# Macaron stack on one core: the position table's copies go from VectorE to ScalarE, its zeros to GpSimd

## The chip, the cores and the metric

The kernel runs on one core of a Trainium2 chip. The metric is the device time of one execution in microseconds (us), the median over several runs. The core has five engines with a queue of instructions each: TensorE (PE, matrix products; its weight loads are shown as PEld), VectorE (DVE), ScalarE (ACT), GpSimd (POOL) and SyncE (SP), which here only starts transfers. An engine takes its instructions in the order of its queue and waits at one whose semaphores have not come. Sixteen DMA engines carry the transfers that SyncE, ScalarE and GpSimd start. SBUF is the memory on the chip, PSUM the small memory that TensorE writes.

## The reference, cut to what matters

Twelve residual steps in four layers, each a mixture of experts, an attention, and the mixture again. All arithmetic is in 32 bits. The change is in layer 0, on x of 4 x 512 rows of 128:

```python
x = L0_attn_x
x = x + 0.5 * _L0_ffn_ref(_layernorm(x, axis=-1), L0_ffn_gate_w, L0_ffn_w1, L0_ffn_b1, L0_ffn_w2, L0_ffn_b2)
x = x + _L0_attn_ref(_layernorm(x, axis=-1), L0_attn_qkv_w, L0_attn_qkv_b, L0_attn_proj_w, L0_attn_proj_b, L0_attn_rel_pos_emb)
x = x + 0.5 * _L0_ffn_ref(_layernorm(x, axis=-1), L0_ffn_gate_w, L0_ffn_w1, L0_ffn_b1, L0_ffn_w2, L0_ffn_b2)
...
```

`_L0_ffn_ref` is the first mixture: a gate picks one of 8 experts for each row, an expert takes at most 320 rows (`CAP0`), multiplies with w1 (128 x 512), adds b1, takes the ReLU, multiplies with w2 and adds b2. `_L0_attn_ref` is a causal attention of 16 heads that adds to each score a number which depends on the head and on the distance between query and key alone; that number is a sum over `L0_attn_rel_pos_emb`.

## The kernel before, in words

**The table.** The attention reads these added numbers from one SBUF tile, `table`, of 128 partitions x 16 heads x 512 numbers. It is made once, in `prep_table`, at the start of the program and is first read by the attention of layer 0, at about 126 us. Only the last 256 numbers of each head depend on the weights; the first 256 are zero. `prep_table` is a generator with three parts:

- It starts the load of the embedding rows (L1016).
- It sums them (L1021), turns them with one product (L1023) and sends a row of 384 numbers for each head to DRAM (L1031).
- For two heads at a time, eight times in all, it loads the row from DRAM with a shift of one per partition into a tile `rev` of 256 KB (L1037, started by ScalarE), turns the order of the partitions with one product by `flip` into a PSUM bank `turned` (L1042, TensorE), and copies the bank into `table` (L1043, VectorE). Behind the eight it writes the zeros (L1044, VectorE).

The `rev` tiles come from a ring of five SBUF buffers with the tag "raw", which other staging tiles use too; the `turned` banks come from a ring of eight PSUM banks that the whole program uses.

**Around it.** The first mixture's object is `f00`. `f00.tokens` normalizes the rows, computes the gate's choice on VectorE, and GpSimd scatters the rows to the experts' places in DRAM, 16 indirect transfers (L416) in all. The call order is: the second part of the table in the middle of the choices, then the rest of the choices, then the third part of the table, then the transposition of b1 (`b1`, L570 on TensorE, copied into `b1T` by L571 on VectorE), then two memsets of the attention's padded values `vpad` on GpSimd (L585). All this stands in a block with `tc.manual_schedule` for four engines: within it each of them keeps the order in which the Python program issues the instructions.

Behind the block comes `f00.experts`. There SyncE loads an expert's rows `d` (L447); VectorE computes their way back (`lost`, L472, and `back`, L475); TensorE transposes the rows (L466) and ScalarE copies them into `dT` (L468); TensorE makes the hidden layer in four pieces of 128 x 320 (L490), of which ScalarE applies b1 and the ReLU to two (L494) and VectorE to two (L495), both reading `b1T`; TensorE makes the output (L526, `o`), VectorE adds b2 (L506), ScalarE weights it (L511), and GpSimd scatters the result (L512). These instructions are placed by a scheduler, from its own estimate of times, which also moves some of them ahead of instructions that the program issued earlier: on VectorE the `lost` and `back` of the first three experts stand between the first copy of the table and the second.

Of the kernel before, what the change touches and what calls it, by code (L numbers as in the profile page):

```python
# [9 lines left out]
FP = mybir.dt.float32  # L10
# [7 lines left out]
P = 128  # L18
D = 128
NB, S = 4, 512  # L20
# [4 lines left out]
NH = 16  # L25
# [16 lines left out]
def kernel(ctx: ExitStack, tc: tile.TileContext, a: dict, out: bass.AP):  # L42
    nc = tc.nc
# [5 lines left out]
    stage = ctx.enter_context(tc.tile_pool(name="stage", bufs=5))  # L49
# [3 lines left out]
    def const(shape, name, dtype=FP):  # L53
        return cpool.tile(shape, dtype, name=name, tag=name)

    def bank(name):
        return psum.tile([P, 512], FP, name=name, tag="bank", bufs=8)
# [19 lines left out]
    flip = const([P, P], "flip")  # L77
# [934 lines left out]
    def prep_table(pool):  # L1012


        rel = stage.tile([P, D], FP, name="rel", tag="rel", bufs=1)
        nc.sync.dma_start(rel, a["L0_attn_rel_pos_emb"][P - 1 : 2 * P - 1, :])  # L1016
        yield

        table = pool.tile([P, NH, S], FP, name="table", tag="table", bufs=1)
        tab = stage.tile([P, NH], FP, name="tab", tag="tab", bufs=1)  # L1020
        nc.vector.tensor_reduce(tab, rel.rearrange("p (h d) -> p h d", d=HD), AX.X, ALU.add)  # L1021
        ps = bank("tabT")
        nc.tensor.matmul(ps[:NH, :P], tab, flip, start=True, stop=True)  # L1023
        last = stage.tile([NH, 1], FP, name="tab_last", tag="tab_last", bufs=1)
        nc.vector.tensor_copy(last, ps[:NH, 0:1])
        row = stage.tile([NH, 3 * P], FP, name="tab_row", tag="tab_row", bufs=1)
        nc.vector.memset(row[:, :P], 0.0)
        nc.vector.tensor_scalar(row[:, P : 2 * P], ps[:NH, :P], last, None, ALU.subtract)
        nc.vector.memset(row[:, 2 * P :], NEG)
        rows = dram.tile([NH, 3 * P], FP, name="tab_rows", tag="tab_rows")  # L1030
        nc.sync.dma_start(rows, row)  # L1031
        yield

        for h in range(0, NH, 2):

            rev = stage.tile([P, 2, 2 * P], FP, name=f"rev{h}", tag="raw")
            nc.scalar.dma_start(  # L1037
                rev,
                bass.AP(tensor=rows.tensor, offset=rows.offset + h * 3 * P, ap=[[1, P], [3 * P, 2], [1, 2 * P]]),
            )  # L1040
            ps = bank(f"turned{h}")
            nc.tensor.matmul(ps, flip, rev.rearrange("p h s -> p (h s)"), start=True, stop=True)  # L1042
            nc.vector.tensor_copy(table[:, h : h + 2, S - 2 * P :], ps.rearrange("p (h s) -> p h s", h=2))  # L1043
        nc.vector.memset(table[:, :, : S - 2 * P], 0.0)  # L1044
        l0["table"] = table
        yield

# [558 lines left out]
    ps = bank("gate0T")  # L1606
    nc.tensor.transpose(ps[:, :E], gate0, ident[:E, :E])
    nc.vector.tensor_copy(gate0T, ps[:, :E])
    with tc.tile_pool(name="tables", bufs=1) as tables:
        f00 = Mixture("f00", CAP0, 1)  # L1610
        f00.zeroed(stage, "raw", 5)
        made = prep_table(tables)
        next(made)
        whole(f00.empty())
# [144 lines left out]
```

## Time and profile before

| | |
|---|---|
| median of 3 runs | 1507.65 us (1504.37 to 1510.55) |
| the profiled execution | 1506.45 us, its span 1504.7 us |
| PE busy | 1258.4 us, 84% of the span |
| DVE, ACT, POOL busy | 893.8, 685.7, 691.0 us |
| granted TensorE clock, mean | 0.908 |
| chain that ended last | PE 63%, DVE 13%, POOL 9%, issue 7%, DMA 6%, ACT 2% |
| eight loads of `rev` (L1037) | started from 34.21 to 44.8 us |
| eight copies of `turned` (L1043) | 0.68 us each, from 40.4 to 55.3 us |
| zeros of the table (L1044) | 3.47 us, at 56.8 us |

The span runs from the first instruction to the last; the execution's own time is 1.75 us longer. The chain that ended last is followed back from the last instruction, at each step to what released it, or to the instruction before it on its engine; "issue" is time in which the engine waited for nothing that the profile shows. In a line of the timeline stand the start, the duration from the first to the end of the last of the merged instructions, the engine, the line, the operation, what it writes and reads, and in brackets how long the engine was idle before it and what released it. A `q` behind an engine's name marks the starting of a transfer in its queue.

### The profile page before, as it was taken

What the parts mean: (1) busy time and instruction counts of PE and PEld (TensorE: products, weight loads), DVE (VectorE), ACT (ScalarE), POOL (GpSimd) and SP (SyncE); (2) the same over time, 40 slices, a digit from 0 to 9 for tenths busy, and PEclk for the clock granted to TensorE, in tenths of its full rate; (3) what the DMA queues carried; (4) which work ended last, traced back from release to release, by engine and by line L of the source; (5) the groups of instructions that cost most, each with busy time, mean ns of one, the idle gap of its engine ahead of it and who ended that gap; (6) DMA issues with size and microseconds to landing.
All of it is one profiled execution on the core that took longest, in us unless ns stands there. A gap on an engine that the chain in (4) does not pass through costs nothing.

```text
span 1504.7 us, 28029 instructions
## 1 busy us (share of the span) xinstructions
PE 1258.4 (84%) x10133; PEld 787.1 (52%) x10133; DVE 893.8 (59%) x3105; ACT 685.7 (46%) x1438; POOL 691.0 (46%) x810
## 2 busy tenths in 40 slices
PE   4788999995979989998999766439599999998394
PEld 4465666674756656676655334227453334333273
DVE  5326766663345657777467766634277787773243
ACT  2135867871443367776621213104245555564041
POOL 5346767872433678876432112554502224212343
PEclk9998999996999999999999776759799999999597
DMA  9420240002413884241130000032105000000223
GB/s 254 114 60 12 80 171 13 9 5 74 137 52 61 228 259 136 93 141 31 32 80 3 1 1 0 29 92 79 56 8 184 9 11 5 15 2 15 78 82 108
DMA packets 100657, 106.15 MB, mean 71 GB/s; under 512 B 9084, under 2 KB 73832, under 8 KB 100520
## 3 DMA queue, kind: packets, MB, share of 16 engines
q1 hardware_dynamic: 89576, 88.01, 20.3%
q0 software_dynamic: 6656, 13.22, 2.5%
q10 hardware_dynamic: 4288, 3.15, 0.8%
q8 instruction: 80, 1.31, 0.3%
q14 instruction: 57, 0.47, 0.1%
HBM read 62.49 MB, written 41.85 MB: 69 GB/s over the span
## 4 chain that ended last, share of the span: by engine, by line
PE 63%; DVE 13%; POOL 9%; issue 7%; DMA 6%; ACT 2%; SPq 0%; POOLq 0%; DVEq 0%; ACTq 0%
PE s_a L621 13%; PE t_a L666 9%; PE o_f L526 5%; PE h_f L490 5%; PE acc_a L688 5%; PE acc_a L826 4%; DVE x L1450 3%; PE t_a L621 3%; PE y_f L1419 2%; POOL disp_f L416 2%; PE ot_a L845 2%; POOL res_f L512 2%; PE gu_f L1218 1%; PE gu_f L1219 1%; PE T_f L195 1%
## 5 line engine op out<-in xcount | busy, mean ns | idle before, releaser
L653 POOL TENSOR_SCALAR sc_a<-sc_a,top_a 128x128 f32<-128x128 f32 (+3 forms) x256 | 275.8, 1092 | 88.0 <-DVE top_a L638 53.8
L621 PE MATMUL s_a<-k_a,q_a 32*128 32x512 f32 (+3 forms) x1536 | 265.1, 539 | 6.0 <-DVE top_a L642 4.8
L710 DVE TENSOR_REDUCE low<-s_a 128x1 f32<-128x512 f32 x256 | 163.0, 684 | 42.8 <-PE t_a L621 31.0
L730 ACT ACTIVATE w_a<-t_a 128x512 f32<-128x512 f32 x240 | 131.6, 596 | 107.1 <-PE t_a L621 69.2
L666 PE MATMUL t_a<-ident,sc_a 128*128 128x128 f32 x1280 | 171.6, 279 | 7.4 <-DVE top_a L642 6.7
L512 POOL DMA_INDIRECT res_f<-y_f,back_f x112 | 106.6, 952 | 140.1 <-ACT y_f L511 92.3
L666 PEld LDWEIGHTS t_a<-ident,sc_a 128*128 128x128 f32 x1280 | 142.8, 143 | 42.6 <-issue 15.8
L621 PE MATMUL t_a<-ql_a,k_a 32*128 32x512 f32 x480 | 157.9, 640 | 0.4 <-DVE low L710 0.3
L655 ACT ACTIVATE sc_a<-sc_a,top_a 128x128 f32<-128x128 f32 (+3 forms) x256 | 134.7, 575 | 16.1 <-DVE top_a L642 15.6
L621 PEld LDWEIGHTS s_a<-k_a,q_a 32*128 32x128 f32 x1536 | 94.7, 186 | 74.5 <-issue 39.0
L675 ACT ACTIVATE w_a<-t_a 128x256 f32<-128x256 f32 (+2 forms) x192 | 94.3, 526 | 70.4 <-PE t_a L666 70.0
L416 POOL DMA_INDIRECT disp_f<-n_f,to_f x96 | 94.8, 988 | 51.5 <-issue 37.2
L526 PE MATMUL o_f<-w_l,h_f 128*128 128x128 f32 (+1 forms) x896 | 111.9, 280 | 3.6 <-ACT h_f L494 3.6
L526 PEld LDWEIGHTS o_f<-w_l,h_f 128*128 128x128 f32 (+1 forms) x896 | 103.9, 186 | 12.6 <-ACT h_f L494 5.6
L490 PE MATMUL h_f<-dT_f,w_l 128*128 128x320 f32 (+1 forms) x256 | 106.6, 555 | 2.8 <-ACT dT_f L468 2.8
L172 POOL TENSOR_SCALAR rs_f<-mv_f 128x4 f32<-128x4 f32 (+1 forms) x23 | 5.3, 231 | 203.4 <-DVE mv_f L169 202.9
L688 PE MATMUL acc_a<-w_a,vpad 128*32 128x128 f32 x2560 | 97.7, 278 | 0.6 <-ACT w_a L675 0.6
L677 ACT COPY w_a<-t_a 128x256 f32<-128x256 f32 (+2 forms) x192 | 93.5, 526 | 5.7 <-PE t_a L666 5.7
L642 DVE CUSTOM_DVE_ANT_0 sc_a<-s_a,table 128x128 f32<-128x128 f32 (+3 forms) x128 | 62.3, 487 | 46.8 <-PE s_a L621 35.2
L642 DVE CUSTOM_DVE_ANT_0 sc_a<-s_a,future 128x128 f32<-128x128 f32 (+3 forms) x128 | 62.4, 487 | 46.3 <-PE s_a L621 39.5
L511 ACT ACTIVATE y_f<-o_f,d_f 128x128 f32<-128x128 f32 (+1 forms) x112 | 38.9, 394 | 105.2 <-DVE o_f L506 93.5
L826 PE MATMUL acc_a<-w_a,vpad 128*32 128x256 f32 x1024 | 82.5, 391 | 2.7 <-ACT w_a L730 2.3
(338 smaller groups left out, 2200.6 us busy)
## 6 DMA issues: line engine op xcount, KB each, us to landing
fac_a<-fac_a_sb SPq DMA_DIRECT2D x36, 256.0 KB
disp_f<-zeros_f SPq DMA_DIRECT2D x4, 2080.0 KB
d_f<-disp_f SPq DMA_DIRECT2D x32, 260.0 KB
w_l<-in_L_ffn_w_dram SPq DMA_DIRECT2D x16, 512.0 KB
cb_f<-rows_f SPq DMA_DIRECT2D x16, 512.0 KB
q_a<-fac_a SPq DMA_DIRECT2D x32, 256.0 KB
k_a<-fac_a SPq DMA_DIRECT2D x32, 256.0 KB
r_f<-res_f SPq DMA_DIRECT2D x16, 256.0 KB
```

The source lines that it names most:

```text
L416: nc.gpsimd.indirect_dma_start(out=self.to[c][i0 + t][:, :], out_offset=bass.IndirectOffsetOnAxis(ap=to[:, c, t : t + 1], axis=0), in_=ns[ ...
L490: nc.tensor.matmul(ps[u][:, :cap], w1[:, e, (c + u) * P : (c + u + 1) * P], dT, start=True, stop=True)
L512: nc.gpsimd.indirect_dma_start(out=self.back[e * per + s][:, :], out_offset=bass.IndirectOffsetOnAxis(ap=back[:m, s : s + 1], axis=0), in_ ...
L526: nc.tensor.matmul(po[:m, s, :], h[:, c, s * P : s * P + m], w2[:, e, c, :], start=(c == 0), stop=(c == NC - 1),)
L621: nc.tensor.matmul(ps[:, n0:n1], q[r : r + SLOT, i * P : (i + 1) * P], k[r : r + SLOT, n0:n1], start=True, stop=True)
L653: nc.gpsimd.tensor_scalar(sc, sc, top, None, ALU.subtract)
L655: nc.scalar.activation(sc, sc, AF.Exp, bias=top, scale=-1.0)
L666: nc.tensor.transpose(ps[:, x * n + j * P : x * n + (j + 1) * P], st["sc", u, i, r0 + x][:, j * P : (j + 1) * P], ident,)
L688: nc.tensor.matmul(st["acc", u][r * SLOT : (r + 1) * SLOT, i * P : (i + 1) * P], vpads[b % 2][:, j, g * 4 + r, :], st["w", u, i, r][:, j * ...
L710: nc.vector.tensor_reduce(st["low", u][:, i, c : c + 1], ps, AX.X, ALU.max, negate=True)
L730: nc.scalar.activation(w, ps, AF.Exp)
L826: nc.tensor.matmul(acc[r * SLOT : (r + 1) * SLOT, n0:n1], vpads[b % 2][:, j, g * 4 + r, :], st["w", u, j, r, half] if ("w", u, j, r, half) ...
```

## The change

The eight copies are made by ScalarE instead of VectorE. The loads, which ScalarE starts, are now written in between: the first three before the first product, and each further one behind the copy of the part three before it. The zeros are written by GpSimd, whose place for it is behind the 16 scatters of the mixture and in front of the `vpad` memsets. Products, sizes and buffers are the same.

```diff
-        for h in range(0, NH, 2):
-
-            rev = stage.tile([P, 2, 2 * P], FP, name=f"rev{h}", tag="raw")
+
+        revs = {}
+
+        def fetch(h):
+            revs[h] = stage.tile([P, 2, 2 * P], FP, name=f"rev{h}", tag="raw")
             nc.scalar.dma_start(
-                rev,
+                revs[h],
                 bass.AP(tensor=rows.tensor, offset=rows.offset + h * 3 * P, ap=[[1, P], [3 * P, 2], [1, 2 * P]]),
             )
+
+        for h in range(0, 6, 2):
+            fetch(h)
+        for h in range(0, NH, 2):
             ps = bank(f"turned{h}")
-            nc.tensor.matmul(ps, flip, rev.rearrange("p h s -> p (h s)"), start=True, stop=True)
-            nc.vector.tensor_copy(table[:, h : h + 2, S - 2 * P :], ps.rearrange("p (h s) -> p h s", h=2))
-        nc.vector.memset(table[:, :, : S - 2 * P], 0.0)
+            nc.tensor.matmul(ps, flip, revs[h].rearrange("p h s -> p (h s)"), start=True, stop=True)
+            nc.scalar.copy(table[:, h : h + 2, S - 2 * P :], ps.rearrange("p (h s) -> p h s", h=2))
+            if h + 6 < NH:
+                fetch(h + 6)
+        nc.gpsimd.memset(table[:, :, : S - 2 * P], 0.0)
         l0["table"] = table
```

## The prediction

> **What bounds the kernel now.** I read the page first: TensorE is busy 84% of the span and carries 63% of the chain that ended last. The change touches none of its instructions, so what counts is where the head of the program makes TensorE wait. Next the chain of waits in order of time, for the first 260 us:
>
> ```profile
> 42.86 4.04 DMA disp_f<-n_f,to_f
> 47.48 0.48 SPq L447
> 48.00 3.43 DMA d_f<-disp_f
> 51.81 4.19 DVE table L1043 x7
> 56.00 0.80 issue
> 56.80 3.47 DVE table L1044
> 60.35 0.54 ACT h_f L494
> 60.94 3.66 PE o_f L526 x16
> 64.60 1.08 PE h_f L490 x4
> ```
>
> Columns are start, duration, work. From 51.81 to 60.35 the chain runs through VectorE's table work: seven of eight copies (L1043), a gap, the memset (L1044). The activation behind them (L494) needs b1T, whose copy (L571) stands on VectorE behind the memset. From 60.94 on it is TensorE almost alone. Then the timeline of the same place:
>
> ```profile
> 34.21 10.95 ACTq L1037 DMA_DIRECT2D rev<-tab_rows  x8
> 40.44 0.69 DVE L1043 COPY table<-turned 128x512 f32<-128x512 f32 x1 [4.08 <-issue]
> 43.82 1.82 POOL L585 MEMSET vpad<- 128x2048 f32 x1
> 46.53 1.10 PE L1042 MATMUL turned<-rev,flip 128*128 128x512 f32 x2 [0.91 <-DMA rev<-tab_rows]
> ...
> 50.11 0.16 DVE L472 SCALAR_TENSOR_TENSOR lost_f<-d_f,astray 128x3 f32<-128x3 f32 x1 [8.98 <-DMA d_f<-disp_f]
> ...
> 53.39 0.42 ACT L468 COPY dT_f<-dT_f 128x320 f32<-128x320 f32 x1 [24.70 <-PE dT_f L466]
> 53.87 4.11 PE L490 MATMUL h_f<-dT_f,w_l 128*128 128x320 f32 x8 [0.64 <-ACT dT_f L468]
> ```
>
> VectorE copies turned part 0 at 40.44 and then sits 8.98 us, because the `lost` of the experts stands ahead of the other seven copies and waits for d_f. Meanwhile ScalarE does nothing (24.70 idle) and TensorE has turned all parts by 50.07. The transposes of expert 0 start only at 52.6: they take the bank of part 1, copied by 52.41.
>
> **The change part by part.** The order of instructions on each engine differs only here; TensorE's and SyncE's orders are the same, and everything behind the first expert is as before. So the question is by how much the 60.94 to 64.60 step moves.
>
> *Removed from VectorE*: 8 copies of 0.68 and the memset of 3.47, 8.9 us in all, of which 8.5 lay on the chain (51.8 to 60.3). VectorE is then free at 51.8 and its b1T copy waits for TensorE alone.
>
> *Added to ScalarE*: 8 copies of 128x512 from PSUM. Nearest row: its own copy nT (L321), 0.58. 4.6 us in idle time. But they stand in front of the dT copy (L468), and from the fourth load on every load stands behind a copy. This makes a loop that did not exist: a load is issued when a copy is done, the copy waits for its product, the product for its load.
>
> *The loads*. One-microsecond cuts of the timeline put the eight issues of before at 34.2, 34.6, 35.4, 38.4, 40.4, 42.1, 43.9 and 44.8. The fourth waited only for earlier transfers, the fifth to eighth for products 0 to 3 (ended 40.40, 42.1, 43.86, 44.77). The product of load 5 started at 46.53, of load 6 at 48.11, both by a DMA: L = 4.4 and 4.2 us from issue to use, two or three in flight. I take L = 4.2. Here a rule gives less: the Trainium skill, "DMA: Bandwidth & Descriptors", section "Anatomy of one DMA — SWDGE (gpsimd) path", fits a fixed 2.0 us plus the bytes at 436 GB/s, for 256 KB 2.6 us (an estimate; its fit is of GpSimd's path). The trace has 4.2 with the DMA engines 0.73 to 0.92 busy; the trace decides. The d_f load, issued 47.04 and used 50.11, gives 3.1 as the low end.
>
> With a warm product of 1.1 (46.53 to 47.6) and 0.65 from its end to the next issue: copy 0 ends 41.05, load 3 is issued 41.1 (before: 38.4), product 3 45.3 to 46.4, load 6 issued 47.05, product 6 51.25. Copy 1 ends 42.75, load 4 issued then, product 4 46.95 to 48.05, load 7 issued 48.65, product 7 52.85 to 53.95 (before: to 50.07). Two loads follow one another, so each us of L costs 2 us. Then b1 to 54.2, the dT transposes 0.6 to 54.8, ScalarE's last copy to 54.6, dT copied 54.9 to 55.3, first product of expert 0 at **55.4**. That is 1.5 us later than before (53.87); what is late next is the loads.
>
> *What TensorE then takes*. Before, the eight products took 4.11 us, 0.53 each; in later experts four take 1.24, 0.27 apart. And o_f took 3.66, later 1.98 to 2.05. The windows:
>
> ```profile
> 46.00:50.00 4.00, 2.98 (x6) 0.97 (x7) 0.00 (x0) 0.00 (x0) 1.81 (x2) 1.00 0.87 214
> 50.00:54.00 4.00, 0.99 (x6) 0.60 (x6) 3.03 (x10) 0.42 (x1) 0.00 (x0) 1.00 0.66 193
> 54.00:58.00 4.00, 4.00 (x10) 2.49 (x10) 3.20 (x5) 0.00 (x0) 0.00 (x0) 0.57 0.15 42
> 58.00:61.00 3.00, 0.47 (x4) 0.20 (x2) 2.89 (x4) 1.07 (x3) 0.00 (x0) 0.99 0.00 0
> 61.00:65.00 4.00, 4.00 (x19) 3.84 (x20) 0.81 (x2) 0.30 (x1) 0.00 (x0) 0.58 0.00 2
> ```
>
> First number busy PE, then PEld, DVE, ACT, POOL; the third from the end is the granted clock: 0.57 and 0.58 right after gaps of 2.4 us (50.25 to 52.62) and 2.5 us (58.4 to 60.94). The Trainium skill, "TensorE: Matmul & The Clock Gate", section "Why this matters for your kernels", says that gaps up to about 3 us leave the clock up. Both rows contradict it. By the rule the eight products would be warm whatever the gaps; by the rows it depends on the pauses of 1.5 us at most between products 3 to 7, with TensorE busy some 55% of 44 to 55. The nearest row, 46 to 50, busy 75% with pauses of 0.5 to 0.9, kept full speed (products of 0.59). I take warm and keep cold for the range.
>
> Warm: eight products 55.4 to 57.7, dT of expert 1 to 58.1, VectorE's last h at 58.3, o_f in 2.0 from about 58.2 to **60.2**. Before it ended at 64.6: **4.4 us earlier**. Cold: 55.4 to 59.5, transposes to 60.0, o_f (warm by then) to 62.0: 2.6 earlier. The second gap, 58.4 to 60.94, is gone either way, as b1T is ready.
>
> *The zeros on GpSimd.* Its 128x2048 memset takes 1.82, so 128x4096 some 3.6 (between VectorE's 3.47 and 3.65). It runs 43.8 to 47.4 behind the last scatter; the vpad memsets move to 51.5. GpSimd then idles (17.90 us before its scatter at 65.77, some 61 now), so zero; cover left 10 us. Waits of other engines on GpSimd ask for its last count copy before the scatters, not for a memset. The scatters themselves are not moved.
>
> *SyncE* keeps its order, but the raw weight loads behind d_f wait for products 4 to 7: the last two go out at about 54.2 instead of 51.9, and the next d_f behind them waits for expert 0's y (67.45 before). Zero, cover 9 us.
>
> Sum: 4.4 us. The profiled execution was 1506.45 (span 1504.7, 1.75 around it), 1.2 below the median 1507.65, so 1502.05 against itself and **1503.2** against the median.
>
> **The rivals.**
> *A, half the gain (cold clock or slower loads)*: 0 to 3 us, about 1505.5. For it: TensorE is idle nearly half of 44 to 55. Against: the 46 to 50 row.
> *B, the loads come quickly*: L of 3.1 gives 2.2 more, 6.6 in all, 1501; the rule's 2.6 gives 7.6, 1500. For it: fewer loads overlap, so less contention. Against: L stayed 4.2 for the sixth load, too.
> *C, slower: ScalarE's copy-then-load loop becomes the bound.* The loads behind copies stretch until product 7 ends so late that the mixture begins later than the 8.5 us it saves. Price 2 us per us of L; it decides at L = 4.2 + 4.4/2 = 6.4 warm, 5.5 cold. With cold turned products as well (0.85 more each, two in the row), cold o_f (1.7 more) and L 4.4, it is 64.6 - 65.8 = 1.2 slower, 1508.9. For L of 8, cold: 5.0 slower, 1512.7. For: scatters and d_f share the DMA engines, 0.87 busy in 46 to 50. Against: no load here showed over 4.4.
> *D, it doesn't do what it says*: the loads are "three ahead" only for the first three; with d_f landing up to 51.4 the mixture could not start much before anyway. The order shows the copies off VectorE, so only the size is in doubt.
>
> **How the numbers follow.** Likeliest case (2 to 6 us) 0.55; A 0.20; B 0.15; C 0.10. The three runs spread from 1504.37 to 1510.55, so their median is good to some 1.5 us. A measurement of this kernel tells about 0.5%, 7.5 us, from no change. Faster than that needs B at its end plus a lucky median: 0.10. Slower by it needs L above 9: 0.05. Range: 1507.65 - 7.6 - 1.5 = 1498.5 to 1507.65 + 1.2 = 1508.9, taken as 1509.
>
> **What would show it.** L1044 gone from VectorE; GpSimd's memset of 3.6 at about 44; ScalarE's copies of 0.58 from 40.45 with loads between, the last ending near 54.6; first h_f product at 53 to 56; no gap of 2.5 us before the first o_f, which ends near 60.2 and takes 2.0; a chain that runs through load, product, copy from 38 to 55 instead of VectorE. The prediction is wrong if the first o_f ends after 64.6, if expert 0's products are at 0.53 each, or if the time behind 65 us differs by more than the shift.

## The result, and the profile after

The changed kernel takes 1500.82 us (median of 20 runs, 1497.09 to 1505.29) against 1505.49 us for the kernel before on the same chip (20 runs): ratio 0.9969, 95% interval 0.9956 to 0.9982. That is 4.67 us between the medians; 4.4 had been forecast. In a later group the two were run side by side again, with 1507.88 against 1512.2 us, ratio 0.9970 (0.9953 to 0.9987). Both intervals exclude 1, so the gain is real; it is smaller than the 0.5% that the prediction took as what one measurement can tell from no change. (The ratios come from runs side by side on one chip and are not exactly the quotients of the medians. Medians of different groups cannot be compared: those of the kernel before lie between 1494.83 and 1512.2 us.)

The chain of waits of the changed kernel, in order of time (start, duration, work), over the place where the chain before ran through VectorE:

```profile
41.47 4.42 DMA rev<-tab_rows
45.93 1.14 PE turned L1048 x2
47.16 4.05 DMA rev<-tab_rows
51.35 1.10 PE turned L1048 x2
53.83 4.11 PE h_f L490 x8
58.36 1.98 PE o_f L526 x16
60.34 1.08 PE h_f L490 x4
```

VectorE's copies and zeros are gone from it. What leads to the mixture is now load, product, load, product. Expert 0's h products start at 53.83, where they started before (53.87), and take the same 4.11 us. The whole difference comes behind them: o_f follows at once and takes 1.98 us, where before TensorE stood still for 2.5 us and then took 3.66. The next h product starts at 60.34 instead of 64.60: 4.26 us earlier. The lines of the kernel before for that place:

```profile
60.19 0.13 DVE L571 COPY b1T_l<-b_l 128x32 f32<-128x32 f32 x1
60.94 3.66 PE L526 MATMUL o_f<-w_l,h_f 128*128 128x128 f32 x16 [2.53 <-ACT h_f L494]
```

The timeline of the changed kernel, same execution (start, duration, engine, line, work; in brackets the idle time in front and what ended it):

```profile
39.70 0.59 ACT L1049 COPY table<-turned 128x512 f32<-128x512 f32 x1 [11.00 <-DMA rev<-tab_rows]
39.76 0.37 ACTq L1039 DMA_DIRECT2D rev<-tab_rows  x1
41.41 0.59 ACT L1049 COPY table<-turned 128x512 f32<-128x512 f32 x1 [1.12 <-PE turned L1048]
41.47 0.37 ACTq L1039 DMA_DIRECT2D rev<-tab_rows  x1
44.12 3.53 POOL L1052 MEMSET table<- 128x4096 f32 x1
47.52 1.45 SPq L447 DMA_DIRECT2D d_f<-disp_f  x3
51.98 0.16 DVE L472 SCALAR_TENSOR_TENSOR lost_f<-d_f,astray 128x3 f32<-128x3 f32 x1 [15.81 <-DMA d_f<-disp_f]
52.48 0.59 ACT L1049 COPY table<-turned 128x512 f32<-128x512 f32 x1 [2.24 <-PE turned L1048]
53.33 0.18 DVE L571 COPY b1T_l<-b_l 128x32 f32<-128x32 f32 x1
```

Two readings matter here. The load behind a copy on ScalarE goes out 0.06 us after that copy *starts*, not after it ends. And b1T is copied at 53.33, before the h products begin; in the kernel before it came behind the zeros, at 60.19.

The windows (engine busy times as before; third number from the end is the granted clock):

```profile
50.00:54.00 4.00, 2.02 (x7) 0.94 (x8) 1.07 (x7) 1.25 (x3) 1.57 (x2) 0.99 0.71 203
54.00:58.00 4.00, 4.00 (x10) 2.50 (x10) 0.58 (x2) 1.05 (x2) 0.00 (x0) 0.58 0.49 141
58.00:61.00 3.00, 3.00 (x23) 2.60 (x21) 0.95 (x2) 0.59 (x2) 0.00 (x0) 1.00 0.01 2
```

The h products still run at a clock of 0.58; o_f, with no pause before it, runs at 1.00. Below, a stretch of products at the higher speed (h in 2.4 us) is called warm, at the lower one (h in 3.9 to 4.3 us) cold. One product of the table stands in these views as two records (x2).

The profiled spans differ by more than this place: 1494.6 against 1504.7 us. The lead is 4.3 us at 60 us and 4.7 at the first scores of the attention (120.4 against 125.1), then grows further down, where the two kernels execute the same instructions in the same order. Single executions wander by more than the effect (1497.09 to 1505.29 us in the 20 runs of the change on one chip), and the profiled one was the fastest of the 20. The yardstick below is therefore the moment at which the first sixteen o_f products end, counted from the start of the last scatter (L416), since the head of the program itself shifts by some 2 us between executions.

### The profile page after: what moved, and what is told of

The parts are those of the page before. It is cut to its first block, busy times and chain, and to the rows that moved or that the text cites. A ratio compares the mean times of both kernels' runs of the same rounds, so it can differ in the third digit from the quotient of the medians.

```text
span 1494.6 us, 28029 instructions
## 1 busy us (share of the span) xinstructions
PE 1251.1 (84%) x10133; PEld 778.6 (52%) x10133; DVE 885.9 (59%) x3096; ACT 690.7 (46%) x1446; POOL 696.1 (47%) x811
## 4 chain that ended last, share of the span: by engine, by line
PE 63%; DVE 12%; POOL 8%; issue 7%; DMA 7%; ACT 2%; SPq 0%; POOLq 0%; ACTq 0%; DVEq 0%
PE s_a L621 13%; PE t_a L666 9%; PE h_f L490 5%; PE acc_a L688 5%; PE o_f L526 5%; PE acc_a L826 5%; DVE x L1458 3%; PE t_a L621 3%; PE y_f L1427 2%; PE ot_a L845 2%; POOL res_f L512 2%; POOL disp_f L416 2%; PE T_f L195 1%; POOL rstd_f L173 1%; DMA cb_f<-rows_f 1%
## 5 line engine op out<-in xcount | busy, mean ns | idle before, releaser
L416 POOL DMA_INDIRECT disp_f<-n_f,to_f x96 | 95.1, 991 | 51.7 <-issue 36.7
L642 DVE CUSTOM_DVE_ANT_0 sc_a<-s_a,future 128x128 f32<-128x128 f32 (+3 forms) x128 | 62.3, 487 | 45.5 <-PE s_a L621 40.4
```

What stands on the lines that cost most here:

```text
L416: nc.gpsimd.indirect_dma_start(out=self.to[c][i0 + t][:, :], out_offset=bass.IndirectOffsetOnAxis(ap=to[:, c, t : t + 1], axis=0), in_=ns[ ...
```

## The experiments

The measure just described, for all kernels, from their timelines, in us. "h starts" and "o_f ends" are counted from the start of the last scatter.

| kernel | last scatter | h starts | h takes | o_f ends | gain on this measure | ratio to before (95%) |
|---|---|---|---|---|---|---|
| before | 42.86 | 11.0 | 4.11 | 21.7 | | |
| the change | 43.16 | 10.7 | 4.11 | 17.2 | 4.6 | 0.9969 (0.9956 to 0.9982) |
| change_again | 44.93 | 11.2 | 3.87 | 17.5 | 4.3 | 0.9970 (0.9953 to 0.9987) |
| zeros_gpsimd_only | 43.47 | 11.4 | 4.07 | 17.9 | 3.8 | 0.9967 (0.9956 to 0.9978) |
| copies_scalar_only | 44.74 | 11.8 | 4.01 | 18.2 | 3.5 | 0.9969 (0.9955 to 0.9982) |
| zeros_first_vector | 43.94 | 12.3 | 4.16 | 18.9 | 2.9 | 0.9983 (0.9972 to 0.9994) |
| no_loads_ahead | 43.63 | 38.3 | 4.32 | 45.0 | -23.2 | 1.0169 (1.0139 to 1.0198) |
| four_ahead | 44.46 | 8.5 | 4.00 | 14.9 | 6.8 | 0.9914 (0.9888 to 0.9941) |
| four_ahead_again | 44.94 | 8.9 | 4.11 | 15.4 | 6.3 | 0.9943 (0.9921 to 0.9964) |
| filler | 43.01 | 11.3 | 2.42 | 16.1 | 5.7 | 0.9953 (0.9935 to 0.9971) |
| four_filler | 43.73 | 9.2 | 2.42 | 14.0 | 7.8 | 0.9958 (0.9940 to 0.9977) |
| four_filler_again | 43.73 | 11.2 | 2.42 | 16.1 | 5.7 | 0.9952 (0.9933 to 0.9971) |
| four_warm | 44.21 | 11.1 | 2.42 | 15.9 | 5.8 | 0.9945 (0.9928 to 0.9962) |

Each row is one trace, and every gain is counted against the one trace of the kernel before. Two traces of one kernel lie 0.3 us (the change), 0.5 (four_ahead) and 2.1 us (four_filler) apart, so differences of a few tenths say nothing. The gain lasts: at the first scores of the attention, some 60 us later, every kernel has its gain on this measure or up to 0.5 us more.

### Which part of the change earns the gain?

My theory after the two traces was that the change gained one thing: TensorE's pause in front of the first o_f (2.5 us) and the slow clock behind it (3.66 instead of 1.98, 1.7 us). Together they are 4.2 us. The pause goes as soon as b1T is ready before the h products end, and that does not take the whole edit. The rival: the parts add up.

The zeros alone go to GpSimd:

```diff
-        nc.vector.memset(table[:, :, : S - 2 * P], 0.0)
+        nc.gpsimd.memset(table[:, :, : S - 2 * P], 0.0)
```

> One part alone: the table's zeros go to GpSimd, the eight copies and the loads stay as in the kernel before. Measured by the moment at which the first sixteen o_f products end (64.60 us before, 60.34 after the whole change). Theory 'one gap': what the change gained is the 2.5 us pause of TensorE before the first o_f and the cold clock behind it (3.66 instead of 1.98), and it goes as soon as b1T is ready before the h products end at 58. Here VectorE's copies end near 56.0 and b1T follows at once, so the h products run 53.9 to 58.0, o_f about 58.4 to 60.4: the whole 4.2 us with half of the edit. Rival 'parts add up': the copies on VectorE still hold up b1T or VectorE's own activations, o_f begins at 59.5 or later and ends past 62: 2.6 us or less of the gain. Median against before: -4.2 us by the first, -2 by the second.

Its timeline:

```profile
44.43 3.53 POOL L1044 MEMSET table<- 128x4096 f32 x1
52.42 4.27 DVE L1043 COPY table<-turned 128x512 f32<-128x512 f32 x7
54.90 4.07 PE L490 MATMUL h_f<-dT_f,w_l 128*128 128x320 f32 x8 [0.64 <-ACT dT_f L468]
56.61 0.18 DVE L571 COPY b1T_l<-b_l 128x32 f32<-128x32 f32 x1
59.32 2.05 PE L526 MATMUL o_f<-w_l,h_f 128*128 128x128 f32 x16
```

All seven copies are still on VectorE, 52.42 to 56.69. But b1T is there at 56.8, before the h products end at 59, and o_f runs without a pause and warm. Median 1501.55 us against 1506.39, 4.8 us: by the medians as much as the whole change, by the traces 3.8 of its 4.6 us.

The other part alone: the change, with the zeros left on VectorE. They stand in its order where the copies were, and run in its idle time.

```diff
-        nc.gpsimd.memset(table[:, :, : S - 2 * P], 0.0)
+        nc.vector.memset(table[:, :, : S - 2 * P], 0.0)
```

> The other part alone: copies on ScalarE with loads three ahead, the zeros stay on VectorE, where they now stand ahead of the wait for d_f (the copies in front of them are gone). Theory 'one gap': VectorE makes the zeros in its idle time before 42, b1T is copied at about 53.3, and the first o_f ends at 60.3 as with the whole change (gain 4.2). Rival 'parts add up': the zeros' 3.5 us still count somewhere, and o_f ends at 62 or later.

Its timeline:

```profile
38.11 3.47 DVE L1052 MEMSET table<- 128x4096 f32 x1 [0.80 <-issue]
55.38 0.19 DVE L571 COPY b1T_l<-b_l 128x32 f32<-128x32 f32 x1 [0.52 <-PE b_l L570]
56.55 4.01 PE L490 MATMUL h_f<-dT_f,w_l 128*128 128x320 f32 x8 [0.64 <-ACT dT_f L468]
60.91 2.05 PE L526 MATMUL o_f<-w_l,h_f 128*128 128x128 f32 x16
```

The zeros run at 38.11, when VectorE had nothing to do, and nobody waits for them. 1501.5 against 1506.39 us, by the medians again the whole gain, by the traces 3.5 us.

The third moves no work to another engine. One line is put ahead of the loop of copies:

```diff
+        nc.vector.memset(table[:, :, : S - 2 * P], 0.0)
         for h in range(0, NH, 2):
...
-        nc.vector.memset(table[:, :, : S - 2 * P], 0.0)
```

> No work changes its engine: against the kernel before, the line of the zeros on VectorE alone is moved from behind the copies to in front of them. VectorE waits there for product 0 until 40.4 and from 41.1 to 50.1 for d_f, so 3.5 us of zeros fit in front. Theory 'one gap': copies end at 56.0, b1T at 56.1, h products 53.9 to 58.0, o_f ends near 60.4, gain 4.2. Rival 'VectorE's load counts': VectorE must lose the copies too, and o_f ends past 62. If the zeros start late they delay the copy of part 0 by at most 3.5 us, with it load 4, and h begins 1 to 3 us later.

1503.45 us, ratio 0.9983: faster than before, by 2.9 us in the medians and in the trace. That is less than the others by both, but its interval overlaps with theirs. Its timeline:

```profile
53.49 0.16 DVE L472 SCALAR_TENSOR_TENSOR lost_f<-d_f,astray 128x3 f32<-128x3 f32 x1 [0.91 <-DMA d_f<-disp_f]
53.77 4.27 DVE L1044 COPY table<-turned 128x512 f32<-128x512 f32 x7
54.63 0.29 PEld L466 LDWEIGHTS dT_f<-ident,d_f 128*128 128x128 f32 x2 [4.83 <-issue]
60.76 2.05 PE L526 MATMUL o_f<-w_l,h_f 128*128 128x128 f32 x16
```

The pause before o_f is gone here as well (h takes 56.25 to 60.41, o_f follows). But the transposes of expert 0 wait until VectorE has copied part 1, which stands behind the third `lost` (53.49), and in this execution d_f was loaded late (issued 4.98 us behind the last scatter, 4.14 in zeros_gpsimd_only). The difference, 0.84 us, is nearly all of what this kernel's h starts later than that of zeros_gpsimd_only (12.3 and 11.4): where the order on VectorE keeps that link, a late d_f is paid. Why d_f was late one trace can't tell; in change_again it was issued 4.98 us behind the scatter too.

So the parts do not add up. Each one alone gives 2.9 to 3.8 us of the 4.6 by the traces, and two of them the whole by the medians. Of the 8.5 us of VectorE work that lay on the chain, moving the 3.5 us of zeros to GpSimd earned most of the gain or all of it; moving them only within VectorE's own order earned some 60% of it in the one trace, with the late d_f in it.

### The loop on ScalarE

The forecast's rival C was a loop of load, product and copy on ScalarE. Here it is at its purest. Against the kernel before, copies and zeros change their engine and nothing else is edited; since the loads stay where the program had them, each now stands on ScalarE behind the copy before it:

```diff
             ps = bank(f"turned{h}")
             nc.tensor.matmul(ps, flip, rev.rearrange("p h s -> p (h s)"), start=True, stop=True)
-            nc.vector.tensor_copy(table[:, h : h + 2, S - 2 * P :], ps.rearrange("p (h s) -> p h s", h=2))
-        nc.vector.memset(table[:, :, : S - 2 * P], 0.0)
+            nc.scalar.copy(table[:, h : h + 2, S - 2 * P :], ps.rearrange("p (h s) -> p h s", h=2))
+        nc.gpsimd.memset(table[:, :, : S - 2 * P], 0.0)
```

> Copies on ScalarE, zeros on GpSimd as in the change, but no load ahead: each load stands behind the copy before it. This shows what the loop of load, product and copy on ScalarE costs. If a load goes out only when the copy in front of it has ended: eight times (L of 3.4 to 4.2, product 1.1, copy 0.6) is 5.1 to 5.9 each, last product at 34.2 + 8 x 5.5 = 78 (75 to 81). If a load goes out while the copy in front of it still runs (the change's trace has issue and copy start 0.00 to 0.06 us apart): eight times (L + 1.1), 4.5 to 5.3, last product at 70 to 77. The first o_f then ends 6.4 us behind it, at 76 to 87, and the time is 12 to 23 us over that of the kernel before; a rival says that other work (weights, d_f) fills the wait so that it is slower by less than 8.

The chain of waits, three turns of it and the last product:

```profile
52.42 3.15 DMA rev<-tab_rows
55.71 2.06 PE turned L1042 x2
57.86 3.16 DMA rev<-tab_rows
61.06 2.09 PE turned L1042 x2
63.23 3.56 DMA rev<-tab_rows
66.92 2.06 PE turned L1042 x2
...
78.04 2.05 PE turned L1042 x2
```

1530.85 us (4 runs) against 1506.39: 24.5 us slower. A turn is load and product alone, 5.4 to 6.0 us; the copy's 0.59 is not in it, because the next load goes out as the copy starts. The last product ends at 80.1. That lies in the range given for the other reading (75 to 81) and past the one given for this (70 to 77), so the end alone would have told the wrong story; the trace decides. The estimate fell short because it had the product at 1.1 us, and it takes 2.06 where TensorE is busy some 38% of the time (2.06 of 5.4). The rival that other work fills the wait fell.

Next, one turn less instead of more: four loads ahead.

```diff
-        for h in range(0, 6, 2):
+        for h in range(0, 8, 2):
             fetch(h)
...
-            if h + 6 < NH:
-                fetch(h + 6)
+            if h + 8 < NH:
+                fetch(h + 8)
```

> The whole change, but with loads four ahead instead of three, which takes one turn of load and product out of ScalarE's loop. Theory 'two chains meet': in the change's trace the last turned product ends at 52.45 and the last d_f load is used at 51.98, so d_f is next; the last product moves to 49 to 50.5, but the transposes of expert 0 start no earlier than 52 and h at 53.3: the first o_f ends 0.3 to 0.7 us earlier, about 17.0 us behind the start of the last scatter instead of 17.4; nothing that the median can tell from the change. Rival 'the loads are the chain': h starts with the last product, 2 us earlier, o_f ends at 58.3 and the median falls by 2 more.

Here my number was wrong (17.0 us) and the rival's came out (15.1 by its 58.3; measured 14.9), though not by its mechanism: h does not start with the last product. From the timeline:

```profile
47.20 2.81 PE L1048 MATMUL turned<-rev,flip 128*128 128x512 f32 x6 [1.28 <-DMA rev<-tab_rows]
48.99 1.45 SPq L447 DMA_DIRECT2D d_f<-disp_f  x3
51.71 0.61 PE L466 MATMUL dT_f<-ident,d_f 128*128 128x128 f32 x3 [1.52 <-DMA d_f<-disp_f]
52.95 4.00 PE L490 MATMUL h_f<-dT_f,w_l 128*128 128x320 f32 x8 [0.64 <-ACT dT_f L468]
```

The products end at 50, and the transposes wait 1.5 us more for d_f, as I had thought. But d_f comes 2.7 us after its issue, not 4.5: in the change the last load of the table went out 0.36 us ahead of d_f (47.16 and 47.52) and d_f took 4.46. In change_again it was 0.52 ahead, and d_f took 4.32. In the five profiles with four ahead the last table load goes out some 4 us or more ahead of d_f, and d_f took 2.66 to 2.83. Over all 13 profiles it is the same: 4.32 to 4.64 us in the three with a table load 0.36 to 0.52 us in front of d_f, 2.66 to 3.12 in the other ten. So the table's last loads appear to cost twice: as a chain of their own, and by slowing d_f. h starts 8.5 us behind the last scatter instead of 10.7.

The first six runs gave 0.9914 (10.9 us between the medians), more than the 6.8 us of this place. Once more, with the unaltered change beside it (no edit in either):

> The changed kernel once more, unaltered, so that it shares its chip and its runs of the kernel before with the two versions beside it. By its trace (first o_f ends 17.2 us behind the start of the last scatter, 21.7 before) the ratio is 0.9970, 4.5 us.

> Loads four ahead, once more with more runs. By its first trace the first o_f ends 14.9 us behind the start of the last scatter, 6.8 earlier than before and 2.3 earlier than in the change: ratio 0.9954, and 0.9985 of the change. Its first six runs gave 0.9914: if that is so, something behind the first mixture gains 4 us more, and the trace must show it behind 65 us. I expect 0.995.

1504.44 us, against 1507.88 for the change and 1512.2 before: ratio 0.9943, 7.8 us, with an interval (0.9921 to 0.9964) that takes in the 6.3 us of its trace (0.9958). Against the change it is 3.4 us by the medians (7 and 16 runs; the intervals of the two ratios overlap) and 2.1 by the traces. What the first ratio has beyond that no trace here explains: at the first scores of the attention the lead of the first trace is 7.3 us. With six runs it may be chance.

### The clock of expert 0's h products

The change leaves h at 4.11 us, 0.53 each, at a clock of 0.58. Two causes were weighed: TensorE had been idle for a good part of the 10 us before, or the 1.4 us between the last product and h. An extra matmul in front of each of the products 3 to 7, overwritten by the product, fills most of TensorE's waits for the loads and leaves the 1.4 us as they are (the `h` of this loop counts heads in steps of two; it is not the hidden layer):

```diff
             ps = bank(f"turned{h}")
+            if h >= 6:
+                nc.tensor.matmul(ps, flip, xs[0].rearrange("p t d -> p (t d)"), start=True, stop=True)
             nc.tensor.matmul(ps, flip, revs[h].rearrange("p h s -> p (h s)"), start=True, stop=True)
```

> The whole change, with one more matmul (the flip against rows of x, 128x512) in front of each of the turned products 3 to 7, into the same bank, where the product overwrites it: TensorE is busy while it waits for the loads. Theory 'the clock follows how busy TensorE was': the eight h products of expert 0, 4.11 us at a granted clock of 0.58 after a stretch with TensorE half busy, run warm in 2.3 us, and the first o_f ends 1.8 us earlier, 15.6 us behind the start of the last scatter instead of 17.4. Rival 'the pause of some 1.4 us in front of h does it': h stays at 4.1 us and the end does not move, or comes up to 1 us later because a product waits behind its filler.

The stretch of 46 to 54 in the change, then in filler, then the one behind it in filler:

```profile
46.00:54.00 8.00, 5.26 (x13) 1.76 (x14) 1.07 (x7) 2.77 (x5) 5.51 (x5) 0.99 0.65 175
46.00:54.00 8.00, 7.22 (x19) 2.89 (x18) 1.07 (x7) 2.55 (x5) 5.37 (x5) 1.00 0.64 171
54.00:58.00 4.00, 3.73 (x19) 2.81 (x20) 1.10 (x2) 1.70 (x4) 0.00 (x0) 1.00 0.55 160
```

Filler's last product ends at 52.88 and h starts at 54.27: the pause, with 0.64 us of transposes in it, is the same 1.4 us. The clock over h is now 1.00 instead of 0.58, and h takes 2.42 us. So that last pause alone does not decide. o_f ended at 16.1 us, not at the 15.6 expected, because h also started 0.6 us later than in the change.

A rival remains: the longest single pause anywhere before h, 1.73 us in the change and only 0.64 in filler. Two other profiles speak against it, four_ahead_again (first two lines) and four_filler_again (last two):

```profile
49.55 2.27 PE L1048 MATMUL turned<-rev,flip 128*128 128x512 f32 x4 [0.74 <-DMA rev<-tab_rows]
53.82 4.11 PE L490 MATMUL h_f<-dT_f,w_l 128*128 128x320 f32 x8 [0.64 <-ACT dT_f L468]
48.96 1.13 PE L1050 MATMUL turned<-rev,flip 128*128 128x512 f32 x2 [0.79 <-DMA rev<-tab_rows]
54.96 2.42 PE L490 MATMUL h_f<-dT_f,w_l 128*128 128x320 f32 x8 [0.64 <-ACT dT_f L468]
```

In the 8 us ahead of h the longest pause is 0.74 us in the first and h is cold; it is 0.79 in the second and h is warm. (The pauses end 4.3 and 6.0 us ahead of h, so a rule on pauses that looks back less than 6 us is not excluded.) The busy share of TensorE over these 8 us sorts the two: 65% and 82%. The change had 64%, four_ahead 57%, both cold; filler had 87%, four_filler and four_warm 92%, all warm. If the share is what counts, the bound lies between 65 and 82% of such a stretch, where it was run at full clock (in copies_scalar_only TensorE was 83% busy from 46 to 54, at a clock of 0.57, and h was cold). How long the stretch is that counts, no run here tells.

Both together (four_filler, the two diffs above), and in four_warm, against four_filler, three extra matmuls in front of the last product:

```diff
-            if h >= 6:
+            for _ in range(0 if h < 6 else 3 if h + 2 == NH else 1):
                 nc.tensor.matmul(ps, flip, xs[0].rearrange("p t d -> p (t d)"), start=True, stop=True)
```

> Four loads ahead and the five extra matmuls together. If both theories of the single kernels hold (d_f bounds the start of h at about 53.3, the busy stretch keeps the clock): the products end near 51, TensorE then pauses 1.5 us for d_f, h runs warm, and the first o_f ends 15.3 us behind the start of the last scatter, 2.1 earlier than in the change. If a pause of 1.5 us is enough to lose the clock, h stays at 4.1 and it is 17.0.

> As with four loads ahead and extra matmuls, but three of them in front of the last turned product, so that TensorE is busy until d_f has landed (products end at about 52 to 53). Theory 'busy before means warm': h runs in 2.3 us and the first o_f ends 15.3 to 15.8 us behind the start of the last scatter. If h is cold in the kernel with one extra matmul each and warm here, then it is the last pause and not the share of busy time that decides. If h is cold in both, neither sets it. The price if the extra matmuls run past d_f: up to 1 us.

> Loads four ahead with the five extra matmuls, once more with more runs. By its first trace the first o_f ends 14.0 us behind the start of the last scatter, 7.7 earlier than before: ratio 0.9949, 0.9 us under the kernel without the extra matmuls. If it is no faster than that kernel, the extra matmuls lose elsewhere what the warm h products win.

h takes 2.42 us in all three. In the first trace o_f ends 14.0 us behind the last scatter, the earliest of all. In four_warm the extra matmuls push the last product to 52.90, past the first d_f (52.48), and h starts at 11.1 instead of 9.2, the price that was named. In four_filler_again the loads of d_f went out 7.3 us behind the last scatter instead of 5.0. The waits of SyncE's queue there (who waited for what: total, times, longest):

```profile
SPq L447 <- DMA disp_f<-n_f,to_f: 3.7, 2, 2.5
SPq L447 <- PE turned L1049: 2.2, 1, 2.2
```

By this the d_f load waited 2.2 us for an extra matmul (L1049). The first profile of the same kernel names no such wait, so the cause stays open. The medians, 0.9958 and 0.9952, are no better than four loads ahead alone (0.9914 and 0.9943). The extra matmuls are not shown to add to four loads ahead. That version has the lowest ratios, but its intervals overlap with those of the kernels with extra matmuls, and on one chip the two lie at 1504.44 and 1505.16 us: these runs do not rank them.

## Why the prediction was right, and where it was not

**The gain and its place: right.** 4.4 us was the sum, 4.26 is what the trace shows at the step it named (60.34 instead of 64.60; forecast 60.2), 4.67 and 4.3 the medians. The mechanism of the main part held: the second pause goes, and o_f runs warm in 2.0, because b1T no longer waits for the table. (It does not wait for TensorE alone, as was written: it stands on VectorE behind the third `lost` and `back`, which wait for d_f until 53.05. At 53.33 it is early enough.) In the prediction's own terms the 4.4 was about the pause (2.5) and the cold o_f (1.7), less 1.5 for a late h, plus 1.8 for a warm h. The first two came, 4.2 us together. Of the other two neither came; that they cancelled was luck.

**The start of h: 1.6 us off.** Forecast 55.4, measured 53.83. The term that failed is "0.65 from its end to the next issue": the load was put behind the end of the copy. It goes out as the copy starts, so the term is 0.05, and it enters twice in a row. The first products also ended 0.7 us sooner (product 0 at 39.7 instead of 40.4), because the first load was used 3.4 us behind its issue instead of 4.1. Why is not shown: zeros_gpsimd_only, with the loads of the kernel before, has 3.45 too. That is 0.7 + 2 x 0.6 less; L, at 4.46 and 4.19 us against the 4.2 taken, gave some 0.3 back.

**The clock over h: 1.8 us off, the other way.** I took warm (2.3) on the strength of the stretch from 46 to 50; it was cold (4.11), rival A's clock. The row tells the clock during a stretch that was 75% busy, not the one behind it; the 8 us that h really followed were 64% busy, less than in any warm case above. The two errors cancelled, and so the sum looks better than its parts. Cold and with the load term right, it would have been 4.2 us by its own working; warm with that term right, 6. By the prediction's own signs it was also wrong here: expert 0's products at 0.53 each were named as such a sign, and they came. Another sign, a time behind 65 us that differs by more than the shift, shows in the first pair of profiles (spans 10.1 us apart) but not in the medians.

**The two rules weighed.** Neither served here. The estimate of 2.6 us for a 256 KB load, made from a figure for GpSimd's path, is under every load by ScalarE that a product waited for: 3.2 to 3.9 us in no_loads_ahead, with one table load in flight, and 4.0 to 4.5 in the change. And TensorE lost its clock over pauses of 1.7 us at most between the last products of the change, where the rule on pauses allows about 3; by the profiles above, the busy share over the 8 us in front sorts warm from cold, and the longest pause in them does not.

**What cost nothing.** The zeros on GpSimd took 3.53 us at 44.12, with the scatters before them: nothing, as said. SyncE's later weight loads: nothing. What I missed there is d_f: the table's loads, now spread to 51, stretched its transfer from 3.07 to 4.46 us. In the change this hid behind the last product (52.45), by half a microsecond.

**The rivals.** C exists, but it takes the loads out of their lead: 24.5 us in no_loads_ahead. With three ahead the longest L was 4.8 us (change_again, load 4: issued 43.42, used 48.17), and C's point was 5.5 to 6.4. B, quick loads, did not come about by quicker loads; four loads ahead reaches its time by another way.

**Not seen at all:** that either half was nearly enough. The prediction took the 8.5 us of VectorE on the chain as one block. A look at when b1T was needed (by about 58, the end of h) against when it came (60.3) would have told that some 2.5 us of VectorE's work had to go, and that the rest of the edit would buy little: 0.8 us by the traces over the zeros alone, nothing by the medians.

## What to carry to other kernels

Price a removal by what becomes late next: the gain was the pause (2.5 us) and the cold clock behind it (1.7), and moving one 3.5 us memset to GpSimd gave nearly all of it. When loads are put into an engine's order behind its computation, count how deep they were before: the old loop already ran four ahead by its buffers, and "three ahead" gave a turn away that four ahead brought back (about 2 us). Look at the busy share of TensorE over several us before a burst (8 here), not only at the last gap, to tell whether the burst runs warm.

## What was unexpected of the hardware

A DMA issued from ScalarE's queue behind a copy went out 0.00 to 0.06 us after that copy started, in all profiles with such loads; it does not wait for the 0.59 us of the copy that it doesn't depend on. A load of 195 KB that went out 0.4 to 0.5 us behind one of 256 KB took 4.3 to 4.6 us instead of 2.7 to 3.1.

The clock column can read 1.00 over slow products. In no_loads_ahead, with TensorE idle some 62% of the time, a turned product took 2.06 us instead of 1.1, and the column read 1.00 from 42 to 65 (first line: a stretch with one such product). In the kernel before (second line) products 0, 1 and 2 ended 1.7 us apart and the two after them 0.9, and the column read 1.00 over the slow ones as well, with TensorE 92% busy:

```profile
54.00:58.00 4.00, 2.05 (x2) 0.50 (x2) 0.00 (x0) 0.20 (x1) 0.00 (x0) 1.00 0.15 45
38.00:42.00 4.00, 3.67 (x5) 1.60 (x6) 0.69 (x1) 0.00 (x0) 3.11 (x5) 1.00 0.92 235
```

So the duration of the matmul is to be read beside the column. That these products were slow by the clock is likely from the factor of about two; no run shows it apart.
